# Respacing the side steps of a fused attention and feed-forward kernel

## The chip, the cores and the metric

The kernel runs on one core of one Trainium2 chip. The metric is device time in microseconds (us); lower is better. The time before is the median of three runs, 1308.55 us (1306.65 to 1314.96).

The engines in the text: PE (TensorE, matmuls), DVE (VectorE), ACT (ScalarE), POOL (GpSimd) and SP (SyncE, which here only issues transfers). Each works through its own instructions in the order in which the program lists them, and waits where data or a buffer is missing.

## The reference, cut to what matters

Inputs are x (4 x 1024 x 256, float32), attention weights, and ternary feed-forward weights w1, w2 (1024 x 256), h1, h2 (1024 x 1024) and w3 (256 x 1024) with a scale for each output.

```python
x = x + layernorm(attention(layernorm(x)))      # 16 heads of 16, softmax over 1024 keys
x = x + layernorm(ffn(layernorm(x)))

def attention(x):
    q, k, v = split(x @ Wqkv.T)
    scores = q @ k.T / sqrt(16)
    e = exp(clip(scores - max(scores), -50, 50))
    return ((e / (sum(e) + 1e-6)) @ v) @ Wout.T

def ffn(x):
    h = silu(x @ w1.T * w1s) * (x @ w2.T * w2s)
    h = gelu(h @ h1.T * h1s)
    h = gelu(h @ h2.T * h2s)
    return h @ w3.T * w3s
```

The small term 1e-6 stands beside a sum of exponentials relative to the row's maximum. The kernel takes exponentials without subtracting the maximum, so it needs the largest exponential of each row: these are the "maxima" below.

## The kernel before

**Attention.** The 16 heads form NG = 4 groups of 4 heads, and the 1024 queries form NH = 2 halves of NQ = 512. The list `tiles` runs over batch b, group g, half h, block c of 128 keys (NT = 8), and u, a pair of heads. That makes 512 tiles. For each tile PE makes the scores s of two heads (128 keys by 2 x 512) and ACT takes their exponential into a ring of RING = 8 tiles (`exponentials`). For each two tiles PE multiplies by the values into acc (`weigh`; one such pair is a block of the weighing), and DVE keeps a running maximum in `top` (`rise`). Sixteen tiles make one unit (b, g, h).

At the end of a unit (`unit_end`) DVE copies acc to `o`, and `divide` brings the maxima into the form that the division needs: SP sends `top` to DRAM (`top_d`), SP brings it back folded over more partitions (`back`, tile `folded`), DVE reduces it further (`fold`), and PE and DVE transpose `o` and divide (`run`; PE writes the one bank `misc`, whose next user must wait until DVE has read it).

**Turns.** The main loop goes by turns of TURN = 3 tiles: three score tiles, then one or two blocks of weighing (so that the number alternates), then one call of `side.take`. All other work of attention is cut into `Step`s in chains that `Side` holds. A step has a gap: it is taken at the earliest that many turns after the step ahead of it in its chain. In one `take`, at most one step with matmuls (`tensor`) is taken over all chains, and chains are asked in order, those of the unit ends first. A unit's chain is added before the take of its own turn, so a gap of 1 means that turn. A `heavy` step is one with a projection; a `patient` one isn't taken right after another heavy step. `next_is_heavy` lets the loop hold back a second block of weighing where a heavy step is due and the ring has room.

**The chains.**

- `prologue(b + 1)` works ahead for the next batch: layernorm (`norm`), normalised rows and their transposes into xT (`xt`), projections to q and k of the first 8 heads (`qk[0]`), values (`v`), then q and k of the last 8 heads (`qk[1]`, not patient there). The results go to the tiles `cq`. `flags` steps compute bounds that decide whether a slower general kernel has to run afterwards.
- `stack(b, g)` copies one group's rows of `cq` (high and low halves) into the operands of the score matmuls, `sk` for keys and `sq` for queries: 32 transfers on SP, for the group after the next. The call comes at the end of a group's half 1. `few` packs several transfers into one step with a gap of 1. `outstanding` lists stacks that aren't complete, and `later["qk1"]` is the batch whose last 8 heads are projected.
- `load_rest` loads later batches of x, wo and the scales, on SP, behind the first stack.
- `round_weights` reads the feed-forward weights, rounds them on POOL and stores them; SP loads them back at the end of attention (`load_weights`), w1, w2 and w3 into the `cq` tiles that have become free.
- `ending(b, h)` follows the last unit of a half: transposes, the projection by wo (py, tile y), layernorm and the residual sum. For the last unit it also calls `open_ffn`, which takes the feed-forward buffers and loads h2.

SP's queue is strictly in order. The lines that matter: stack copies are issued at L418, `top_d` at L505, `folded` at L508, later weights at L740. The fold is L512 on DVE, the transposes of `o` L517 and of `folded` L520 on PE. Score matmuls are L470, exponentials L471, weighing L478, maxima L487, the division L492 to L495. Projections (p, pv, py) are matmuls at L264, copies out of PSUM are L267 (ACT) and L270 (DVE), and transposes are L306 (pt) and L555.

**Feed-forward.** Eight halves go through `gated` (w1, w2), `gelu_layer` (h1, then h2) and `finish` (w3). The first calls `side.take` after each of its 8 column blocks, which is where the last units' endings are done.

Of the kernel before, what the change touches and what calls it, by code (L numbers as in the profile page):

```python
# [116 lines left out]
def tile_fast(ctx: ExitStack, tc: tile.TileContext, x, wqk, wv, wo, w1, w1s, w2, w2s, h1, h1s, h2, h2s, w3, w3s, out, bad):  # L117
# [62 lines left out]
    with ExitStack() as actx, ExitStack() as rctx:  # L180
# [91 lines left out]
        def prologue(b, space, copy):  # L272
# [122 lines left out]
                    nc.vector.tensor_scalar(misses[0:1, k + i : k + i + 1], most[:, i : i + 1], limit, 0.0, ALU.is_le, ALU.is_equal)  # L395

            norm = [[Step(gather(h, i), 1, False) for i in range(0, TPQ, 2)] + [Step(root(h), 0, False)] for h in range(NH)]
            xt = [[Step(apply(h, i), 1, False) for i in range(0, TPQ, 2)] + [Step(transposes(h, c), 1) for c in range(DC)] for h in range(NH)]
            qk = [[[Step(project(w, m, h), 1, heavy=True) for w in (1, 0)] for h in range(NH)] for m in range(DC)]
            v = [Step(values(t), 1, heavy=b > 0) for t in range(0, NT, 2)]  # L400
            flags = []
# [19 lines left out]

            return [copy(u, j, n) for u in range(2) for j in range(PARTS) for n in range(2)]

        def few(run_all, n=5):


            def some(part):
                return lambda: [run() for run in part]

            return [Step(some(run_all[i : i + n]), 1, False, quiet=True) for i in range(0, len(run_all), n)]  # L430

        def stack(b, g):

            outstanding.append((b, g))

            def done():
                stacked[g % 2] = b, g
                outstanding.remove((b, g))

            steps = few([lambda copy=copy: copy(nc.sync) for w in (1, 0) for copy in copies(g, w)])  # L440
            steps[0].ready = lambda: g < GPT or later["qk1"] == b
            return steps + [Step(done, 0, False, quiet=True)]

# [56 lines left out]
        def divide(g, h, o, top):  # L500


            there = shuffle.tile([HPG, P, P], F32, tag="top", name="top_d")
            folded = work.tile([P, P // SLOT, P], F32, tag="folded", name="folded", bufs=1)
            nc.sync.dma_start(out=there.rearrange("i k q -> k i q"), in_=top.rearrange("p u n q -> p (u n) q"))  # L505

            def back():
                nc.sync.dma_start(out=folded, in_=there.rearrange("i (k s) q -> (i k) s q", s=P // SLOT))  # L508

            def fold():  # L510
                for n in (2, 1):
                    nc.vector.tensor_max(folded[:, 0:n], folded[:, 0:n], folded[:, n : 2 * n])  # L512

            def run():
                p = misc("po")
                for t in range(TPQ):
                    nc.tensor.transpose(p[:, t * P : (t + 1) * P], o[:, t * P : (t + 1) * P], ident)  # L517

                pm = p.rearrange("p (n s) -> p n s", s=SLOT)[:, :, HOLE : HOLE + P // (TPQ * HPG)]
                nc.tensor.matmul(pm, folded[:, 0], ident.rearrange("p (n k) -> p n k", n=TPQ * HPG), start=True, stop=True, is_transpose=True)  # L520
                em = small.tile([P, HPG], F32, tag="em", name="em")
                nc.vector.tensor_reduce(em, pm.rearrange("p (i n) k -> p i n k", i=HPG), AX.XY, ALU.max)
                po = p.rearrange("p (t i s) -> p t i s", t=TPQ, s=SLOT)
                quotients(g, h, em, po)

            return [Step(back, 1, False, quiet=True), Step(fold, 2, False), Step(run, 1)]

        def divide_last(g, h, o, top):

# [14 lines left out]
        def ending(b, h, copy):  # L544

            st = {}

            def transposes(c):
                def run():
                    if c == 0:  # L550
                        st["oT"] = work.tile([P, DC, NQ], F32, tag="oT", name=f"oT_{b}_{h}", bufs=1)
                        st["y"] = (both if h else work).tile([P, TPQ, D], F32, tag="y", name=f"y_{b}_{h}", bufs=1)
                    pt = misc(f"po_{b}_{h}_{c}")
                    for t in range(TPQ):
                        nc.tensor.transpose(pt[:, t * P : (t + 1) * P], on[h][:, t, c * P : (c + 1) * P], ident)  # L555
                    copy(st["oT"][:, c, :], pt)

                return run

            def project(t0):  # L560
                def run():
                    py = misc(f"py_{b}_{h}_{t0}").rearrange("p (t d) -> p t d", d=D)
                    for i in range(2):
                        for c in range(DC):
                            by_slots(py[:, i, :], st["oT"][:, c, (t0 + i) * P : (t0 + i + 1) * P], wo_sb[:, c, :], start=c == 0, stop=c == DC - 1)
                    (copy if b == B - 1 else to_scalar)(st["y"][:, t0 : t0 + 2, :], py)

                return run

            def gather(i):  # L570
                def run():
                    st["mv"] = norms.gather([st["y"][:, j, :] for j in range(i, i + 2)], i, st.get("mv"))

                return run

            def root():
                st["ln"] = norms.root(st["mv"])

            def apply(i0):
                def run():  # L580
                    for i in range(i0, i0 + 2):
                        norms.apply(st["y"][:, i, :], st["y"][:, i, :], st["ln"], i)

                return run

            def residual(i):
                def run():
                    xr = xs[b][:, h * TPQ + i : h * TPQ + i + 2, :]
                    nc.vector.tensor_add(xr, xr, st["y"][:, i : i + 2, :])

                return run

            return (
                [Step(transposes(c), 1) for c in range(DC)] + [Step(project(t), 2 if t else 1, heavy=True) for t in range(0, TPQ, 2)]
                + ([Step(open_ffn, 0, False)] if (b, h) == (B - 1, NH - 1) else [])
                + [Step(gather(i), 1, False) for i in range(0, TPQ, 2)] + [Step(root, 0, False)]
                + [Step(apply(i), 1, False) for i in range(0, TPQ, 2)] + [Step(residual(i), 1, False) for i in range(0, TPQ, 2)]
            )
# [90 lines left out]
        def unit_end(b, g, h):  # L689

            o = both.tile([P, NQ], F32, tag="o", name="o", bufs=2)
            to_vector(o, accs[b, g, h])

            assert g or not b or not any(step.tensor for step in ends[b - 1, h][0])
            unit = side.add((divide_last if (b, g) == (B - 1, NG - 1) else divide)(g, h, o, tops[b, g, h]), True)
            if g == NG - 1:
                last = ending(b, h, to_scalar if (b, h) == (B - 1, NH - 1) else to_vector)
                for step in last:
                    step.patient = False
                unit[0].extend(last)  # L700
                ends[b, h] = unit
            if h < NH - 1:
                return

            n, at = g + 2, b
            if n >= NG:
                n, at = n - NG, b + 1
            if b == B - 1 and g == NG - 2:
                side.add([Step(lambda c=c: load_weights("h1", [c]), 2 if c else 0, False, quiet=True) for c in range(HC // 2)])
            if at < B:  # L710
                put = Step(slots(at, n), 0, False)
                if at > b:
                    assert later["qk"] == at
                    later["chain"][0].append(put)
                else:
                    put.run()
                side.add(stack(at, n))
            if g == NG - 3 and b + 1 < B:
                later["chain"][0].extend(later["rest"])
            elif g == NG - 3:  # L720
                chunks = [(n, [c]) for n in ("w1", "w2") for c in range(DC)] + [("w3", range(c, c + 4)) for c in range(0, HC, 4)]
                side.add([Step(lambda n=n, c=c: load_weights(n, c), 2, False, quiet=True) for n, c in chunks])
                side.add([Step(lambda: None, 7, False)] + prepare(0, to_vector))
            if g == NG - 1:
                begin(b + 1)
# [16 lines left out]
        def open_ffn():  # L742
# [3 lines left out]
            ffn["b"] = halves(fb, "hb")  # L746
            homes["h2"] = [fb.tile([P, HID], F32R, name=f"h2_{c}") for c in range(HC)]
            load_weights("h2")

        def norm_steps(tiles, st):  # L750

# [227 lines left out]
        early = [v[1], Step(slots(0, 0, 0, NT // 2), 0, False)]  # L979
        side.add(early + v[2:] + [Step(slots(0, 0), 0, False), Step(slots(0, 1), 0, False)] + sum(qk[1], []) + [Step(lambda: later.update(qk1=0, v=0), 0, False), Step(lambda: add_flags(flags[0] + flags[1]), 0, False)])  # L980
        begin(0)
        side.add(stack(0, 1) + few(load_rest(), 4))
        side.add([s for k in blocks for s in round_weights(*k)])
        made = seen = weighed = 0

# [7 lines left out]
        while weighed < len(tiles):  # L993
            n = end = made
            end += TURN
            make(end)
            if made == len(tiles):
                n = made
# [16 lines left out]
            make(end)  # L1015
            if weighed < len(tiles):
                left = 2 * (NT - tiles[weighed][3])
                side.take(left <= min(4, made - weighed))

        load_weights("h1", range(HC // 2, HC))  # L1020
# [239 lines left out]
```

## Time and profile before

| what | us |
|---|---|
| median of three runs | 1308.55 |
| lowest, highest | 1306.65, 1314.96 |
| the profiled execution, own time | 1312.02 |
| its span, first to last instruction | 1310.2 |
| PE busy | 1247.4 |
| ACT busy | 723.2 |
| DVE busy | 701.3 |
| POOL busy | 118.0 |

The granted PE clock is 0.987 on the mean. Attention lasts to about 635 us, and the feed-forward part takes the rest. A row of a timeline gives start, length, engine and source line, the operation, its output and inputs by tile name, the shapes and a count; a bracket at its end holds the engine's idle time just ahead of it and what ended it. "SPq" is SP's queue issuing a transfer. A row of the stretches gives the window, its length, and for each engine its busy time and count, then PE's granted clock, the busy share of the transfer engines, and GB/s. A row of waits gives the waiting engine, tile and line, what it waited for, the total in us, how many times, and the longest.

### The profile page before, as it was taken

To read this page: it belongs to the slowest core of one execution; us is meant where nothing else is said; L and a number is where in the kernel's file an instruction comes from. 1 tells how busy PE (TensorE), PEld (TensorE's weight loads), DVE (VectorE), ACT (ScalarE), POOL (GpSimd) and SP (SyncE) were. 2 spreads that over 40 slices of the span, in tenths; PEclk is the share of its full clock that TensorE was granted. 3 is DMA by queue.
4 is the path that set the end of the run, shared out by engine and by line. 5 is a ranking of instruction groups with operands and counts; after the bars stand their busy time and mean duration, and the time that the engine had idled before them with its cause. 6 is when DMAs were issued, how large, how long until landed. Compare 5 with 4: busy or idle time off the path is not lost.

```text
span 1310.2 us, 21118 instructions
## 1 busy us (share of the span) xinstructions
PE 1247.4 (95%) x8104; PEld 770.6 (59%) x8104; DVE 701.3 (54%) x1578; ACT 723.2 (55%) x902; POOL 118.0 (9%) x166
## 2 busy tenths in 40 slices
PE   7997999999999999988999999999999999999995
PEld 3332333333333333323588888888888888888885
DVE  3364457764487445646663634647446474463533
ACT  3886889889898988988521422314223142231410
POOL 6220113112030000000000000000000000000000
PEclk8998999999999999999999999999999999999998
DMA  4674556566554444455220000201102011020000
GB/s 128 175 225 111 149 137 171 146 143 176 117 146 97 88 98 98 84 121 167 81 113 1 25 1 1 65 25 33 57 1 65 25 33 57 1 65 9 17 1 20
DMA packets 65678, 107.02 MB, mean 82 GB/s; under 512 B 12960, under 2 KB 39200, under 8 KB 65568
## 3 DMA queue, kind: packets, MB, share of 16 engines
q1 hardware_dynamic: 57680, 80.93, 25.2%
q0 software_dynamic: 7360, 24.12, 5.9%
q8 instruction: 66, 1.08, 0.4%
q10 hardware_dynamic: 528, 0.52, 0.1%
q14 instruction: 44, 0.36, 0.1%
HBM read 48.38 MB, written 23.59 MB: 55 GB/s over the span
## 4 chain that ended last, share of the span: by engine, by line
PE 68%; DVE 10%; DMA 7%; ACT 6%; SPq 5%; issue 2%; ACTq 0%; POOL 0%; POOLq 0%; DVEq 0%
PE ph L796 36%; PE acc L478 10%; PE s L470 7%; SPq L418 5%; PE pz L849 4%; ACT e L471 4%; PE pg L796 3%; PE p L264 3%; DMA folded<-top_d 3%; PE py L264 2%; DVE sg L812 2%; DMA top_d<-top 2%; DVE ha_lo L801 1%; PE pv L264 1%; DVE st L95 1%
## 5 line engine op out<-in xcount | busy, mean ns | idle before, releaser
L471 ACT ACTIVATE e<-s 128x1024 f32<-128x1024 f32 x512 | 483.9, 1036 | 45.7 <-PE s L470 26.2
L478 PE MATMUL acc<-e,vaug 128*32 128x512 f32 x2048 | 257.4, 605 | 0.9 <-POOL vaug L448 0.7
L832 ACT ACTIVATE a<-ph,h_scale 128x512 f32<-128x512 f32 x128 | 81.0, 685 | 300.9 <-PE ph L796 300.9
L470 PE MATMUL s<-sq,sk 64*128 64x512 f32 x1024 | 186.0, 446 | 18.7 <-ACT e L471 12.6
L796 PE MATMUL ph<-hb_hi,h 128*128 128x512 f32 x512 | 199.5, 390 | 0.0
L796 PE MATMUL ph<-hb_lo,h 128*128 128x512 f32 x512 | 199.4, 390 | 0.0
L470 PEld LDWEIGHTS s<-sq,sk 64*128 64x128 f32 x1024 | 86.2, 186 | 137.1 <-ACT e L471 108.5
L487 DVE TENSOR_TENSOR top<-top,e 128x512 f32<-128x512 f32 x192 | 135.3, 705 | 18.3 <-ACT e L471 12.2
L478 PEld LDWEIGHTS acc<-e,vaug 128*32 128x32 f32 x2048 | 49.5, 109 | 108.3 <-issue 104.1
L105 POOL TENSOR_TENSOR rstd<-ve,minus_half 128x4 f32<-128x4 f32 (+1 forms) x33 | 36.8, 1114 | 793.3 <-DVE ve L103 793.3
L796 PEld LDWEIGHTS ph<-hb_lo,h 128*128 128x128 f32 x512 | 96.1, 188 | 20.1
L796 PEld LDWEIGHTS ph<-hb_hi,h 128*128 128x128 f32 x512 | 96.1, 188 | 20.2
L833 DVE CAST ha_hi<-a 128x512 fp32r<-128x512 f32 x64 | 27.1, 424 | 141.8 <-ACT a L832 141.8
L796 PE MATMUL ph<-ha_hi,sq 128*128 128x512 f32 x256 | 101.7, 397 | 0.4
L796 PE MATMUL ph<-ha_lo,sq 128*128 128x512 f32 x256 | 99.9, 390 | 0.0
L796 PE MATMUL ph<-ha_lo,sk 128*128 128x512 f32 x256 | 99.8, 390 | 0.0
L796 PE MATMUL ph<-ha_hi,sk 128*128 128x512 f32 x256 | 99.7, 390 | 0.0
L810 ACT ACTIVATE sg<-pg,w_scale 128x512 f32<-128x512 f32 x64 | 43.3, 688 | 55.0 <-DVE ha_lo L801 43.3
L812 DVE SCALAR_TENSOR_TENSOR sg<-pg,w_scale,sg 128x512 f32<-128x512 f32 x64 | 47.1, 745 | 48.3 <-ACT sg L810 48.3
L264 PE MATMUL p<-xT,wqk_sb 128*32 128x512 f32 x512 | 62.4, 609 | 2.5 <-DVE on L495 1.0
L833 DVE CAST hb_hi<-a 128x512 fp32r<-128x512 f32 x64 | 27.0, 422 | 69.0 <-ACT a L832 69.0
L796 PEld LDWEIGHTS ph<-ha_hi,sq 128*128 128x128 f32 x256 | 48.1, 188 | 12.7 <-DVE sg L812 3.3
(164 smaller groups left out, 1637.2 us busy)
## 6 DMA issues: line engine op xcount, KB each, us to landing
w<-in_h_dram POOLq DMA_DIRECT2D x16, 512.0 KB, 6.4
h_r<-wr POOLq DMA_DIRECT2D x16, 512.0 KB, 4.0
x<-in_h_dram SPq DMA_DIRECT2D x32, 256.0 KB, 2.6
top_d<-top SPq DMA_DIRECT2D x30, 256.0 KB, 2.5
folded<-top_d SPq DMA_DIRECT2D x30, 256.0 KB, 3.2
sk<-ck1hi SPq DMA_DIRECT2D x64, 64.0 KB, 2.7
sk<-ck1lo SPq DMA_DIRECT2D x64, 64.0 KB, 2.5
sq<-cq1hi SPq DMA_DIRECT2D x64, 64.0 KB, 2.4
```

Of the source, the lines that this page charges most:

```text
L264: nc.tensor.matmul(o[j : j + SLOT, :], w[:, j : j + SLOT], i, **flags)
L418: queue.dma_start(out=stacks[w, i, u][o : o + DH, c0:c1].bitcast(F32), in_=cq[w, m, k][r : r + DH, c0:c1].bitcast(F32))
L470: nc.tensor.matmul(s[:, a, :], stacks[1, g % 2, u][r, c * P : (c + 1) * P], stacks[0, g % 2, u][r, h * NQ : (h + 1) * NQ], start=True, sto ...
L471: nc.scalar.activation(pair(k)[:, u], s, AF.Exp)
L478: nc.tensor.matmul(acc[SLOT * i : SLOT * (i + 1), :], vaug[g % 2][:, c, i, :], pair(k)[:, i // 2, i % 2, :], start=c == 0, stop=c == NT - 1)
L487: nc.vector.tensor_max(top, top if c > 1 else pair(k - 2)[:, :, :, 0:P], pair(k)[:, :, :, 0:P])
L796: nc.tensor.matmul(p, homes[n][c][:, m * P : (m + 1) * P], half[:, c, :], start=c == 0 and k == 0, stop=c == len(homes[n]) - 1 and k == 1)
L810: nc.scalar.activation(sg, p[:, 0, :], AF.Silu, scale=scales["w1"][:, m : m + 1])
L812: nc.vector.scalar_tensor_tensor(sg, p[:, 1, :], scales["w2"][:, m : m + 1], sg, ALU.mult, ALU.mult)
L832: nc.scalar.activation(a, p[:, j, :], AF.Gelu, scale=scales[n][:, m : m + 1])
L833: nc.vector.tensor_copy(o[0][:, m, :], a)
L849: nc.tensor.matmul(p[t], half[:, c, t * P : (t + 1) * P], homes["w3"][c], start=c == 0 and k == 0, stop=c == HC - 1 and k == 1)
```

## The change

- The transposes into xT come two turns after the normalisation (first of each half), not one; the first projection by wo comes two turns after the transposes, not one.
- A stack's 32 copies go by 4 in a step, not 5, or by 6 where the last 8 heads of the batch are needed and not yet projected when the stack is called for. `load_rest` goes by 1 in a step, not 4.
- `back` comes a turn later.
- What was an assertion on the first unit of the next batch becomes a condition on its `run`: it waits for the matmul steps of the ending of the batch before.
- w1's loads wait until the flag steps are done, w2's until no stack is outstanding, and w3's move into `open_ffn`, behind those of h2.
- After a turn that weighed two blocks or more, patient heavy steps aren't taken.

```diff
-  xt = ... [Step(transposes(h, c), 1) for c in range(DC)]
+  xt = ... [Step(transposes(h, c), 1 if c else 2) for c in range(DC)]

   # stack(b, g)
-  steps = few([... for w in (1, 0) for copy in copies(g, w)])              # n=5
+  steps = few([... for w in (1, 0) for copy in copies(g, w)], 4 if g < GPT or later["qk1"] == b else 6)

   # divide
-  return [Step(back, 1, False, quiet=True), Step(fold, 2, False), Step(run, 1)]
+  return [Step(back, 2, False, quiet=True), Step(fold, 2, False), Step(run, 1)]

   # ending
-  [Step(project(t), 2 if t else 1, heavy=True) for t in range(0, TPQ, 2)]
+  [Step(project(t), 2, heavy=True) for t in range(0, TPQ, 2)]

   # unit_end
-  assert g or not b or not any(step.tensor for step in ends[b - 1, h][0])
   unit = side.add(..., True)
+  if b and not g:
+      unit[0][-1].ready = lambda: not any(step.tensor for step in ends[b - 1, h][0])
   ...
-  chunks = [(n, [c]) for n in ("w1", "w2") for c in range(DC)] + [("w3", range(c, c + 4)) for c in range(0, HC, 4)]
-  side.add([Step(lambda n=n, c=c: load_weights(n, c), 2, False, quiet=True) for n, c in chunks])
+  chunks = [(n, [c]) for n in ("w1", "w2") for c in range(DC)]
+  loads = [Step(lambda n=n, c=c: load_weights(n, c), 2 if n == "w1" else 1, False, quiet=True) for n, c in chunks]
+  loads[0].ready = lambda: not later["flags"][0]
+  loads[DC].ready = lambda: not outstanding
+  side.add(loads)

   # open_ffn
   load_weights("h2")
+  load_weights("w3")

-  side.add(stack(0, 1) + few(load_rest(), 4))
+  side.add(stack(0, 1) + few(load_rest(), 1))

   # the loop over turns
+  before = weighed
   ...
+  side.tired = side.tired or weighed - before >= 4
   side.take(left <= min(4, made - weighed))
```

More of the change, by code (lines that the diff above doesn't have):

```diff
@@ L397, in prologue @@
             norm = [[Step(gather(h, i), 1, False) for i in range(0, TPQ, 2)] + [Step(root(h), 0, False)] for h in range(NH)]
-            xt = [[Step(apply(h, i), 1, False) for i in range(0, TPQ, 2)] + [Step(transposes(h, c), 1) for c in range(DC)] for h in range(NH)]
+            xt = [[Step(apply(h, i), 1, False) for i in range(0, TPQ, 2)] + [Step(transposes(h, c), 1 if c else 2) for c in range(DC)] for h in range(NH)]
             qk = [[[Step(project(w, m, h), 1, heavy=True) for w in (1, 0)] for h in range(NH)] for m in range(DC)]
@@ L422, in copies, with few @@
             return [copy(u, j, n) for u in range(2) for j in range(PARTS) for n in range(2)]
-        def few(run_all, n=5):
+        def few(run_all, n):
             def some(part):
@@ L438, in done @@
                 outstanding.remove((b, g))
-            steps = few([lambda copy=copy: copy(nc.sync) for w in (1, 0) for copy in copies(g, w)])
+            steps = few([lambda copy=copy: copy(nc.sync) for w in (1, 0) for copy in copies(g, w)], 4 if g < GPT or later["qk1"] == b else 6)
             steps[0].ready = lambda: g < GPT or later["qk1"] == b
@@ L593, in ending @@
             return (
-                [Step(transposes(c), 1) for c in range(DC)] + [Step(project(t), 2 if t else 1, heavy=True) for t in range(0, TPQ, 2)]
+                [Step(transposes(c), 1) for c in range(DC)] + [Step(project(t), 2, heavy=True) for t in range(0, TPQ, 2)]
                 + ([Step(open_ffn, 0, False)] if (b, h) == (B - 1, NH - 1) else [])
```

## The prediction

> **What bounds the kernel now.** I read the busy rows first, then the busy time by stretches, the chain of waits, the list of waits, and the timeline round the longest stops. A *unit* below is one (batch, group, half); it is over when its 16th tile is weighed. "h0" and "h1" are its two halves.
>
> ```profile
> PE 1247.4 (95%) x8104; PEld 770.6 (59%) x8104; DVE 701.3 (54%) x1578; ACT 723.2 (55%) x902; POOL 118.0 (9%) x166
> PE   7997999999999999988999999999999999999995
> ACT  3886889889898988988521422314223142231410
> ```
> ```profile
> 80.00:120.00 40.00, 31.17 (x218) 10.90 (x214) 19.19 (x40) 28.53 (x34) 4.78 (x6) 0.87 0.64 164
> 280.00:320.00 40.00, 38.07 (x374) 15.27 (x372) 20.40 (x48) 36.54 (x44) 7.41 (x11) 1.00 0.66 163
> 680.00:720.00 40.00, 40.00 (x190) 33.52 (x189) 13.05 (x26) 8.09 (x13) 0.00 (x0) 1.00 0.00 0
> ```
> There are two regimes. From 635 us on (feed-forward) PE has no gap (40.00 of 40), and the change hardly touches that part. From 27 to 632 us (attention) PE and ACT are both near full (38.1 and 36.5 of 40 at 280), so a stop of either is lost to the end. The stretch at 80 is the poorest: both engines lose 7 to 8 us against 280, and PE's granted clock is 0.87 there.
>
> ```profile
> PE ph L796 36%; PE acc L478 10%; PE s L470 7%; SPq L418 5%; PE pz L849 4%; ACT e L471 4%; PE pg L796 3%; PE p L264 3%; DMA folded<-top_d 3%; PE py L264 2%; DVE sg L812 2%; DMA top_d<-top 2%; DVE ha_lo L801 1%; PE pv L264 1%; DVE st L95 1%
> ```
> ```profile
> DVE folded L512 <- DMA folded<-top_d: 41.3, 15, 7.7
> PE po L520 <- DVE folded L512: 12.0, 4, 7.8
> PE s L470 <- DMA sq<-cq1lo: 2.8, 1, 2.8
> ```
> The chain passes through SP's issue of stack copies (L418, 5%), then through the maxima's way out (top_d, 2%) and back (folded, 3%). DVE stands 41.3 us for the maxima, and PE 12.0 us behind DVE. The timeline shows how:
>
> ```profile
> 100.94 2.49 SPq L418 DMA_DIRECT2D sq<-cq1lo  x4
> 103.48 0.58 SPq L418 DMA_DIRECT2D sq<-cq1hi  x1
> 104.16 0.53 SPq L505 DMA_DIRECT2D top_d<-top  x1
> 106.73 0.33 SPq L508 DMA_DIRECT2D folded<-top_d  x1
> 109.60 0.75 DVE L512 TENSOR_TENSOR folded<-folded 128x256 f32<-128x256 f32 x2 [7.67 <-DMA folded<-top_d]
> 110.40 0.47 PE L520 MATMUL po<-ident,folded 128*128 128x128 f32 x1 [7.79 <-DVE folded L512]
> 111.69 2.85 ACT L471 ACTIVATE e<-s 128x1024 f32<-128x1024 f32 x3 [7.55 <-issue]
> 112.38 3.56 PE L478 MATMUL acc<-e,vaug 128*32 128x512 f32 x16
> ```
> The unit (b0, g1, h0) was done at 92.64 (copy of acc to o), yet SP sent top_d only at 104.16, behind a row of copies at 0.62 us each (2.49 / 4). In all 15 h0 units that were profiled with top_d, SP sent it 0.1 to 11.5 us after o (median 3.0); in the 15 h1 units 2.7 us before to 0.6 after. SP's queue is late in h0 units only, because the 32 copies of the next stack start at the h1 end before them.
>
> **What the stops cost.** I sorted the 170 turns by what PE does in them and took the median of each kind; a turn's excess is its length less that median. Excesses at the stops of the maxima: (b0,g0,h0) 0.93 + 1.05 = 1.98; (b0,g1,h0) 11.58 against 3.75, then 5.66 against 3.57, = 9.92; (b0,g2,h0) 5.27 against 3.45 = 1.82 (PE waits for DVE's read of the misc bank, DVE for folded, 5.33). For (b3,g1,h0) the neighbours without projections give 5.79 per two turns: 9.28 - 5.79 = 3.49. The sum is 17.2. The last stack's late landing (below) took 7.88 for two such turns: 2.09. Together **19.3 us**. ACT's idle at the same places is 1.81 + 1.44, 7.55 + 2.55, 1.90, 1.94 + 1.02 and 1.57, 19.8 us, so no other engine gained meanwhile and I count it in full.
>
> After the 7.79 us gap the next 16 acc matmuls took 3.50 us to the next instruction, against 1.85 elsewhere; after the 2.20 us gap at 557 they took 2.56. Both are inside the excesses. The Trainium skill ("TensorE: Matmul & The Clock Gate", What's actually happening) has PE's clock halved after about 3.4 us idle. By that rule the second would not be slow; the trace has it slow, and by the rule the sum would be 0.7 less.
>
> **The change, part by part.**
>
> *Stacks by 4 a turn (6 only where a batch's second half of q and k is not ready at the call).* The same 32 copies, 0.63 us each. Five turns (mean (631.94 - 27.27) / 170 = 3.56 us) lie between the h1 end and the next h0 end. Before, 25 copies stood ahead of top_d there; now 20 do: 5 x 0.63 = 3.15 us earlier, which is the median lateness. Four a turn need 2.5 us of a turn's 2.75 to 3.6; five needed 3.15. The case of six: only b1's fourth projection (PE at 235.7) falls in the turn of the unit end, so one stack (b1,g2); its unit (b1,g1,h0) stays as late as now, its excess of 0.82 is not in my sum.
>
> *The rest of the loads by 1 a turn, not 4.* Between 79.45 and 104.16 the queue also held 11 of these transfers (2 of wo, 4 of x, 5 of scales) beside the copies. Now each turn holds one step (0.57 us for a wo piece): 20 x 0.63 + 5 x 0.57 = 15.5 from 77.1 gives 92.6, when the maxima are ready. 25 steps from turn 9 on end near 30 + 34 x 3.56 = 150 us; wo is first used at 199.6, x of batch 2 after 200. Nothing is late.
>
> *back a turn later.* back, fold and run go from turns 0, 2, 3 after the end to 1, 3, 4. On SP, 4 copies (2.5 us) now stand between top_d and back, which hides top_d's landing (2.5 us) instead of blocking the queue. On DVE, fold comes 3.56 us later. Ready: o + 0.8 + 0.5 + 2.5 + 0.4 + 3.2 (at most 5.4) = 7.4 to 9.6 us after the end; wanted: three turns, 8.7 to 10.7. So DVE's 41.3 us goes to at most 1 us in a few units, and PE, a turn behind fold, feels none. run then ends 4 turns after the end, before the next unit's 5.33; the o, top and folded buffers are not needed sooner.
>
> *xt transposes, and the first y projection, gap 2; the ready condition on the next batch's first run.* The same instructions a turn later. Removed: PE's waits there, 0.10 + 0.47 + 0.17. The prologue has slack: b3's q and k were projected by 425, wanted at 460. The next batch's first run comes 15 turns after the ending starts, so its condition is already true. At the end, the last y projections move up to two steps into the first gate stage, and with them the eight h2 loads (landed 667.7, wanted at 688): two steps of 2.3 to 3.9 us are covered. Price 0.
>
> *No patient heavy step in a turn of two blocks.* Of ten heavy steps behind two blocks in the trace, one (59.2) is patient; the others are second-half q/k, y and batch 0's v. PE's work is the same; -0.5 to +0.5, taken as 0.
>
> *w1, w2, w3.* Before, w2's load stood in the middle of the last stack:
>
> ```profile
> 593.34 0.33 SPq L740 DMA_DIRECT2D cq1hi<-w_r  x1
> 593.71 1.14 SPq L418 DMA_DIRECT2D sq<-cq1lo  x2
> 598.50 0.93 PE L470 MATMUL s<-sq,sk 64*128 64x512 f32 x4 [2.77 <-DMA sq<-cq1lo]
> ```
> It overwrites cq, so it waited for copies to land, and two copies waited behind it. Now w2 waits until no stack is outstanding: copies go out by 583.5 + 0.5 + 2.5 + 0.4 + 2.5 = 589.4 and land near 592, before 595. That is the 2.09. w2 is wanted at 635 and comes near 600. w3's eight loads follow h2's: 8 x 0.48 after 660, wanted at 717. Hidden by the h1 layer.
>
> *What it may cost anew.* Every moved step meets other neighbours on DVE and in the one misc bank. PE's gaps behind late DVE work (norm, xT, on, oT, ck0lo), beside those counted, are ten, 8.2 us in all. The change could clear them all (+8.2) or add as many (-8.2). No row says which; I take two new ones of 1 us: -2.0.
>
> **Sum:** 19.3 - 2.0 = 17.3 us. The profiled execution took 1312.02 (span 1310.2, 1.8 around it), so 1294.7; the median of the runs shown is 3.5 lower, 1308.55, and gives **1291.2**. (1%, 13.1 us, is about what a measurement of this kernel can tell from no change.)
>
> **Rivals.**
> - *A wait takes the place:* fold and run fall on busier DVE turns and the 8.2 us of late DVE gaps double. 19.3 - 8.2 = 11.1: 1297.5. For it: four such gaps at po L517 already lie beside maxima that came in time. Against: fold itself no longer blocks DVE.
> - *The maxima still land late:* half the stops stay: 19.3 / 2 - 2.0 = 7.7: 1300.9. For it: folded took 5.1 to 5.4 us in four units while 512 KB loads ran. Against: that fits in three turns. The Trainium skill ("DMA: Bandwidth & Descriptors", Issuing engines are not separate DMA queues) speaks for it: transfers of all issuers share the same 16 engines, so four copies sent behind top_d slow it. The trace agrees in that top_d, 2.5 us in the middle, took 4.6 at 600 with large loads in flight.
> - *Slower: stacks land late.* The last four copies come in the eighth turn, not the seventh. The first s of a group found its stack landed only 0.70 to 3.87 us before (14 groups, 33.7 in all). If landing slips by one turn and half of back's stop (5.0 us), PE stands 14 x 5.0 - 33.7 = 36.3 us: 1291.2 + 36.3 = 1327.5. It decides from a slip of 3.6 us (17.1 us of stops). Against: SP isn't paced by turns; copies run at 0.63 us each, and by the count above they end sooner.
> - *More than counted:* the 8.2 us goes as well: 25.5: 1283.0. For it: (b1,g0,h0) had 1.72 of excess behind fold's 0.96.
>
> **How the numbers follow.** Forecast 0.48 (own range 1285 to 1298), a wait in its place 0.20, late maxima 0.12, late stacks 0.10, more 0.10. Faster by over 1% (under 1295.5): 0.85 x 0.48 + 0.10 + a quarter of 0.20 = 0.56. Slower by over 1%: late stacks and a little, 0.11. Within: 0.33. The range reaches below the best case (1283) and to the late maxima with the 8.2 us added (1300.9 + 8.2): 1281 to 1309.
>
> **What would show it.** Right: DVE's wait for folded under 8 us in all, no PE wait at L520, top_d of h0 units sent within 1 us of o, the window 80 to 120 at clock 1.00 and 37 us of PE, no wait of s for sq<-cq1lo, the feed-forward part as long as before (675 us). Wrong: first s of groups waiting for sk or sq; po L517 or py waiting for DVE by more than 15 us; the attention part ending after 625 us.

## The result, and the profile after

The changed kernel takes 1303.33 us (median, 1300.64 to 1306.56), the kernel before 1308.22 us on the same chip. The ratio is 0.9956, 95% interval 0.9942 to 0.9970: a gain of 4 to 8 us, real but within 1%. The prediction was 1291.2, a gain of 17.3. The profiled execution took 1304.9 us with a span of 1303.1, so between the two profiles the span lost 7.1.

First the busy rows, the stretches and the chain of the kernel after. In the feed-forward part its source lines lie 6 further down.

```profile
PE 1246.2 (96%) x8104; PEld 771.5 (59%) x8104; DVE 700.2 (54%) x1578; ACT 721.6 (55%) x902; POOL 119.4 (9%) x166
```
```profile
80.00:120.00 40.00, 35.41 (x258) 12.63 (x248) 20.47 (x42) 32.96 (x38) 7.11 (x9) 0.91 0.61 142
280.00:320.00 40.00, 39.17 (x362) 15.15 (x360) 20.64 (x47) 37.70 (x45) 7.58 (x10) 1.00 0.65 162
```
```profile
PE ph L802 36%; PE acc L478 12%; ACT e L471 8%; PE s L470 8%; PE pz L855 4%; PE pg L802 4%; PE p L264 4%; PE py L264 2%; PE pv L264 2%; DVE sg L818 2%; PE po L517 1%; DVE ha_lo L807 1%; DVE top L487 1%; DVE st L95 1%; ACT sg L816 1%
```
SP's copies (5% of the chain before), top_d (2%) and folded (3%) no longer stand among the chain's largest lines: of the stop that the change attacks, little is left in what sets the end. The stretch at 80 is better (PE 31.2 to 35.4 of 40) but not well: its granted clock is still 0.91.

The list of waits (engine, tile and line, what it waited for: total us, times, longest us) shows what is left and what is new:

```profile
DVE folded L512 <- DMA folded<-top_d: 12.5, 5, 5.4
PE po L517 <- DVE cq0lo L330: 3.6, 1, 3.6
PE po L555 <- DVE oT L270: 2.0, 1, 2.0
PE s L470 <- DMA sq<-cq1lo: 1.9, 1, 1.9
PE py L264 <- DVE norm L362: 1.7, 1, 1.7
```
DVE's wait for the maxima fell from 41.3 to 12.5 us, and PE's 12.0 us at L520 is gone. In its place PE waits for DVE at transposes and projections: 3.6, 2.0 and 1.7 us here, and 1.6, 1.4 and 1.2 in rows further down. The row of s is the stack of (b0, g3), which landed late.

**Where the time went, group by group.** I cut attention at the first score matmul of each of the 16 groups. From batch 1 on such a length hardly varies where the order of the work is the same: the kernel after and experiment e3 below, which differ in batch 0 alone, agree within 0.04 us in all twelve, e15 and e17 in ten. A few times it jumped all the same (against e8, b3 g1 by 1.7 in e13 and e14, and b1 g3 by 1.3 in e14), so a difference of one group below 2 us is used only where several kernels show it. The first gate matmul of the feed-forward part comes at 635.46 us before and 628.68 after; from there to the end it is 674.8 and 674.4.

| us after less before | g0 | g1 | g2 | g3 |
|---|---|---|---|---|
| batch 0 | -2.72 | -6.63 | -1.43 | **+4.27** |
| batch 1 | +0.12 | +0.85 | -1.94 | -1.11 |
| batch 2 | **+2.81** | **+2.91** | -1.59 | +1.14 |
| batch 3 | -0.01 | -1.04 | +0.71 | -2.35 |

The five groups in which the prediction placed its 19.3 us (b0 g0 to g2, b3 g1, b3 g3) gained 14.2. The other eleven lost 8.2, where it had 2.0. Batch 0 gained 6.5 in all, and batches 1 to 3 nothing (+0.5).

Two stops of the kernel after show why. The first is the old one, still there in the worst unit (timeline; "SPq" rows are issues):

```profile
87.51 0.69 DVE L270 TENSOR_SCALAR o<-acc 128x512 f32<-128x512 f32 x1 [0.29 <-PE acc L478]
97.83 0.53 SPq L505 DMA_DIRECT2D top_d<-top  x1
100.46 0.36 SPq L508 DMA_DIRECT2D folded<-top_d  x1
103.24 0.75 DVE L512 TENSOR_TENSOR folded<-folded 128x256 f32<-128x256 f32 x2 [5.37 <-DMA folded<-top_d]
104.07 0.69 DVE L330 SCALAR_TENSOR_TENSOR cq0lo<-p,cq0hi 128x512 fp32r<-128x512 f32 x1
104.82 1.12 PE L517 MATMUL po<-ident,o 128*128 128x128 f32 x4 [3.57 <-DVE cq0lo L330]
```
The copy to o was at 87.51 (first row), so top_d of (b0, g1, h0) went 10.3 us late, with 30 stack copies ahead of it. DVE stood 5.37 us in fold; cq0lo, which frees the misc bank, was queued behind; PE stood 3.57 us for the bank.

The second is new, at the start of batch 2, where no transfer is late:

```profile
363.26 1.21 DVE L349 TENSOR_REDUCE sum<-ck1hi 128x1 f32<-128x1024 f32 x1
364.99 0.42 DVE L95 BATCH_NORM_STATS2 st<-y 128x6 f32<-128x256 f32 x1
366.26 0.69 DVE L270 TENSOR_SCALAR oT<-po 128x512 f32<-128x512 f32 x1
367.00 0.66 PE L555 MATMUL po<-ident,on 128*128 128x128 f32 x4 [2.04 <-DVE oT L270]
372.76 0.75 DVE L512 TENSOR_TENSOR folded<-folded 128x256 f32<-128x256 f32 x2
373.54 0.69 DVE L362 TENSOR_REDUCE norm<-pn 64x4 f32<-64x512 f32 x1
374.29 1.94 PE L264 MATMUL py<-wo_sb,oT 128*32 128x256 f32 x32 [1.68 <-DVE norm L362]
```
The layernorm of y (st<-y) of the ending, the next batch's sums and norm, and a fold fall together on DVE. oT stands behind sum and st, norm right behind a fold (before, this fold ended 0.7 us ahead of norm). Each PE step there needs the misc bank that DVE has yet to read (oT, norm), and waits.

### The profile page after: what moved, and what is told of

Read it like the earlier page. It is cut to its first block, busy times and chain, and to the rows that moved or that the text cites. A ratio compares the mean times of both kernels' runs of the same rounds, so it can differ in the third digit from the quotient of the medians.

```text
span 1303.1 us, 21108 instructions
## 1 busy us (share of the span) xinstructions
PE 1246.2 (96%) x8104; PEld 771.5 (59%) x8104; DVE 700.2 (54%) x1578; ACT 721.6 (55%) x902; POOL 119.4 (9%) x166
## 3 DMA queue, kind: packets, MB, share of 16 engines
q8 instruction: 66, 1.08, 0.3%
## 4 chain that ended last, share of the span: by engine, by line
PE 74%; ACT 10%; DVE 8%; issue 3%; DMA 2%; POOL 1%; SPq 1%; ACTq 0%; POOLq 0%; DVEq 0%
PE ph L802 36%; PE acc L478 12%; ACT e L471 8%; PE s L470 8%; PE pz L855 4%; PE pg L802 4%; PE p L264 4%; PE py L264 2%; PE pv L264 2%; DVE sg L818 2%; PE po L517 1%; DVE ha_lo L807 1%; DVE top L487 1%; DVE st L95 1%; ACT sg L816 1%
## 5 line engine op out<-in xcount | busy, mean ns | idle before, releaser
L470 PE MATMUL s<-sq,sk 64*128 64x512 f32 x1024 | 189.5, 447 | 22.2 <-ACT e L471 17.2
L818 DVE SCALAR_TENSOR_TENSOR sg<-pg,w_scale,sg 128x512 f32<-128x512 f32 x64 | 47.1, 745 | 46.3 <-ACT sg L816 46.1
```

The lines of the kernel that those rows point to most:

```text
L470: nc.tensor.matmul(s[:, a, :], stacks[1, g % 2, u][r, c * P : (c + 1) * P], stacks[0, g % 2, u][r, h * NQ : (h + 1) * NQ], start=True, sto ...
L818: nc.vector.scalar_tensor_tensor(sg, p[:, 1, :], scales["w2"][:, m : m + 1], sg, ALU.mult, ALU.mult)
```

## The experiments

The theory after the result: the maxima's later return is the gain; the y projection's gap takes it back in batches 1 to 3; the rule on two blocks delays a stack in batch 0. Rivals: the gain is the spreading of transfers; the loss is late stacks, or shared transfer engines. All ratios are to the kernel before on the same chip, with their 95% intervals. "Lengths" are those of groups, from the profiled execution.

**1. What brings the gain?** The extra turn alone taken out of the changed kernel (e7), and alone put into the kernel before (e8):

```diff
-            return [Step(back, 2, False, quiet=True), Step(fold, 2, False), Step(run, 1)]
+            return [Step(back, 1, False, quiet=True), Step(fold, 2, False), Step(run, 1)]    # e7; e8 is the reverse, in the kernel before
```


> The changed kernel with the bringing back of the maxima in the unit's own turn again. Theory (the extra turn is what takes the wait off DVE): folded lands 7.4 us after the unit's end at best and fold asks for it after two turns, 5.8 to 7.1, so DVE waits in most h0 units again (10 to 20 us in all), the copies stand behind the landing of the maxima, and the time rises by 3 to 8 us. Rival (with 4 copies a turn SP is in time anyway, the turn was not needed): within 2 us of the changed kernel, or faster, since the division comes a turn sooner.

> The kernel before with nothing but the maxima brought back a turn later. Theory: fold asks 3.6 us later, more than the median lateness of 3.0, so DVE's 41 us of waiting falls to about 10, PE's stop at (b0, g1, h0) from 7.8 to 4, the other stops of PE vanish, and the time falls by 6 to 10 us. Rival (five copies now stand between sending and bringing back, so the maxima come back as late against fold as before): DVE still waits 25 us or more, and the time stays within 3 us.

Measured: e7 1314.92, ratio 1.0022 (1.0000 to 1.0043); e8 1299.22, ratio 0.9907 (0.9873 to 0.9941). The waits of e7, then those of e8:

```profile
DVE folded L512 <- DMA folded<-top_d: 28.9, 10, 8.5
PE po L520 <- DVE folded L512: 8.6, 1, 8.6
```
```profile
DVE folded L512 <- DMA folded<-top_d: 22.1, 7, 6.4
PE po L517 <- DVE xT L270: 4.5, 1, 4.5
```
The one number in `divide` is worth about 12 us alone (e8), twice the whole change, and about 9 us within it (1.0022 less 0.9956); all the rest together, without it, is worth nothing or a little less. DVE still stands 22.1 us in e8, yet PE no longer stands at L520: with one more turn the wait of DVE is absorbed before PE needs it. (For e8, a wait of about 10 us and a gain of 6 to 10 were foretold: the wait fell less and the gain was larger.) That settles against the spreading of transfers as the source.

**2. The gaps.** Both gaps back to 1 in the changed kernel (e4), the xt gap alone back (e5); on top of e8, the xt gap alone (e9), or the projection's gap alone with the ready condition that it needs (e10).

```diff
-... [Step(transposes(h, c), 1 if c else 2) for c in range(DC)]          # e4, e5
+... [Step(transposes(h, c), 1) for c in range(DC)]                      # e9: the reverse, in e8
-... [Step(project(t), 2, heavy=True) for t in range(0, TPQ, 2)]         # e4
+... [Step(project(t), 2 if t else 1, heavy=True) ...]                   # e10: the reverse, in e8
```


> The changed kernel with the gaps of the xT transposes and of the first y projection back at 1. Bunching theory: the moved ending now puts the layernorm of y on DVE in the same turns as the next batch's own layernorm, PE waits behind DVE for the one misc bank (2.0, 1.7, 1.6 and 1.4 us between 365 and 397), and the groups from b2g0 and b2g1 lose 2.8 and 2.9 us. With the gaps back both return to 38.8 and 34.3 us and the time falls by 3 to 6 us. Rival (the later maxima move the ending, not these gaps): both groups stay at 41.6 and 37.3, and the time stays within 2 us.

> The changed kernel with the gap of the xT transposes alone back at 1 (the first y projection stays at 2). With both back the time fell from 0.9956 to 0.9890 of the kernel before, by 8.6 us. Theory of the ending: it is the y projection, a turn later in all eight endings, that puts the layernorm of y beside the next batch's work, and the xT gap acts once a half: at most 2 us here, ratio 0.994 to 0.996. Rival theory of the prologue: the xT gap delays the projections of q and k, and the whole 8.6 us comes back, ratio 0.989.

> The kernel before with the maxima brought back a turn later (that alone gave 0.9907, a span of 1298.2 us) and the xT transposes at gap 2. If this gap is what the whole change lost: the time rises by 3 to 8 us, ratio 0.993 to 0.997. If it is harmless, as the forecast had it (the prologue has slack): within 2 us of 0.9907.

> The kernel before with the maxima a turn later, and the first y projection at gap 2 (with the ready condition that it needs). If the later ending is what meets the next batch's work on DVE: the groups from b2g0 and b2g1 grow by 2 to 3 us each against 38.5 and 35.9, and the time rises by 3 to 8 us. If harmless: within 2 us of 0.9907.

| | ratio (95%) | batch 0, us | batches 1 to 3, us |
|---|---|---|---|
| before | 1 | 164.5 | 443.7 |
| the change | 0.9956 (0.9942 to 0.9970) | 158.0 | 444.2 |
| e4, both gaps undone | 0.9890 (0.9869 to 0.9911) | 150.7 | 438.7 |
| e8, back only | 0.9907 (0.9873 to 0.9941) | 159.9 | 436.6 |
| e9 = e8 + xt gap | 0.9897 (0.9868 to 0.9926) | 157.4 | 436.3 |
| e10 = e8 + projection gap | 0.9938 (0.9916 to 0.9959) | 158.7 | 442.4 |

e10 loses 5.8 us in batches 1 to 3 against e8, at the start of the batches (b1 g0 +1.18, b2 g1 +1.24, b3 g0 +1.08, b3 g1 +0.84), where an ending lies beside the next batch's prologue. Each of these is small, and less than the 2 to 3 us foretold for b2 g0 and b2 g1 (+0.5 and +1.2), but the total stands over all runs: the six kernels with `back` at 2 and the projection's gap at 2 (the change, e1, e2, e3, e5, e10) take 442.4 to 444.4 us in batches 1 to 3, the twelve with it at 1 take 436.3 to 440.7. Undoing both gaps in the changed kernel (e4) gives 5.5 back there, 2.0 and 2.3 of it in b2 g0 and b3 g0.

Group b2 g1 did not follow e4's expectation: it stays at 37.0 (37.25 in the change, 34.3 before). Part of its loss comes with the turn itself (35.9 in e8) and part with the rule on two blocks, which the prediction took as 0: with the projection's gap at 1, b2 g0 and b2 g1 take 39.6 to 39.7 and 37.0 in the four kernels with the rule (e4, e6, e12, e18), and 38.2 to 38.5 and 35.3 to 36.1 in the eight without it. Other groups shorten with the rule (b2 g2 by about 1 us), so its price over these batches is not settled.

The xt gap costs nothing on top of e8 (e9). In the changed kernel the evidence is split. By its times e5, with the xt gap alone undone, is as fast as e4: 1299.24, ratio 0.9898 (0.9865 to 0.9932), which is what the rival foretold. Its profiled execution, however, was the slowest of its eight (1306.06), and in it batches 1 to 3 take 444.4, as in the changed kernel, so no trace shows where the others were faster. The loss in batches 1 to 3 goes with the projection's gap (e9, e15, e16 and e17 have the xt gap at 2 and take 436.3 to 436.9); whether the xt gap costs something more in the changed kernel stays open.

In e10's list of waits stand many short ones of PE for DVE's readings of the misc bank (p for norm 1.6, xT 1.3 and oT 1.2, py for xT 1.1). Over batches 1 to 3 PE stands 3.0 us longer in e10 than in e8 (21.5 and 18.5), 2.7 of it behind DVE, and ACT 5.0 longer (48.2 and 43.2). So half of the 5.8 is read directly as PE waiting for DVE; the other half lies in turns that are longer without a gap that the trace gives to anyone, and no run splits it further.

**3. Batch 0: who sends the maxima late?** In the changed kernel, stacks always by 4 (e1), no rule on two blocks (e2), the rest by 4 again (e3); on top of e8, the rule alone (e12) and the rest by 1 alone (e13).

```diff
-            steps = few([...], 4 if g < GPT or later["qk1"] == b else 6)
+            steps = few([...], 4)                                        # e1
-                side.tired = side.tired or weighed - before >= 4         # e2 (e12: added to e8)
-        side.add(stack(0, 1) + few(load_rest(), 1))
+        side.add(stack(0, 1) + few(load_rest(), 4))                      # e3 (e13: the reverse, in e8)
```


> The changed kernel, with every stack's copies by 4 a turn (never 6). Queue theory: in the changed kernel the stack for (b0, g2) went by 6, because the two-block rule moved the last q/k projection of batch 0 past the unit end; so 30 copies stood ahead of the maxima of (b0, g1, h0), sent 10.3 us late, and DVE stood 5.4 us, PE 3.6, ACT 4.9. With 4 a turn they leave 6 us earlier, DVE's wait there is under 1 us, the group from b0g1's first scores to b0g2's is 3 to 5 us shorter, and the time falls by 3 to 5 us (about 1299). Rival (the stop only moves): the stack of (b0, g2) lands after its first score matmul, and the time stays at 1303.

> The changed kernel without the rule that keeps patient heavy steps out of turns with two blocks. The projection of batch 0 is then done before the unit end again, so that stack goes by 4 of itself. Queue theory: the same gain as with 4 always, 3 to 5 us. Rival (the rule earns its keep elsewhere): the time stays or rises, since turns with two blocks and a projection (4.5 us against 2.75 and 3.6 apart) come back.

> The changed kernel with the remaining loads by 4 a turn again, not 1. Queue theory: spread by 1 they run beside the stacks of (b0, g2) and (b0, g3), and made the latter land 2.9 us after its first score matmul; by 4 they are over by then, the group that begins at b0g3 loses its extra 4.3 us, but the maxima of the first batch's units are sent later again by 4 loads a turn: net -3 to +2 us. Rival (the loads do no harm): the group from b0g3 stays at 40 us.

> The kernel before with the maxima a turn later, and the rule of no patient heavy step in a turn of two blocks. There is no six-a-turn rule here for it to set off. If its harm in the whole change came only from that: within 2 us of 0.9907. If keeping large steps out of full turns is worth something: 2 to 4 us faster; if it delays the projections: slower by as much.

> The kernel before with the maxima a turn later, and the remaining loads by 1 a turn. If spreading them is what helps the first batch: DVE's wait for folded falls below 15 us (22.1 without it), the group from b0g1 falls under 42, and the time is 1 to 4 us below 0.9907. If the loads only move beside later stacks: one of the groups from b0g2 and b0g3 grows by as much, within 2 us of 0.9907.

| | ratio (95%) | (b0, g1), us | (b0, g3), us |
|---|---|---|---|
| the change | 0.9956 (0.9942 to 0.9970) | 41.1 | 40.0 |
| e1, always by 4 | 0.9915 (0.9899 to 0.9932) | 37.1 | 39.1 |
| e2, no rule | 0.9919 (0.9901 to 0.9938) | 36.9 | 37.8 |
| e3, rest by 4 | 0.9964 (0.9952 to 0.9975) | 46.1 | 35.8 |
| e8, back only | 0.9907 (0.9873 to 0.9941) | 43.5 | 36.9 |
| e12 = e8 + rule | 0.9907 (0.9876 to 0.9938) | 48.0 | 35.7 |
| e13 = e8 + rest by 1 | 0.9888 (0.9851 to 0.9924) | 39.5 | 36.8 |

The rule kept batch 0's last q and k projection past the end of the unit (b0, g0, h1), so `stack(0, 2)` was called with the last 8 heads not projected and went by 6. That put 30 copies ahead of top_d, not 20. Without the rule the stack goes by 4 of itself, and SP sends top_d 5.5 us earlier (timeline of e2):

```profile
92.29 0.39 SPq L505 DMA_DIRECT2D top_d<-top  x1
```
e1 reaches the same by the other way. Either gives about 5 us (0.9956 less 0.9915 or 0.9919, of 1308). With stacks by 4 the rule itself costs nothing in (b0, g1) (e1 keeps it, e2 does not), so there its price comes with the stack. On top of e8 the rule nets nothing in time (e12): (b0, g1) is 4.5 longer, but by another stop, that of (b0, g0, h1), whose folded took 8.0 us to land while PE stood 7.9 us; other groups are shorter. The rest by 1 does what was foretold in (b0, g1): 5.0 us in the changed kernel (e3), 4.0 on top of e8 (e13). But against e3 the changed kernel gives 4.2 us back in (b0, g3): by 1, the loads stretch over the next stack too. That does not happen always: with the loads by 1 too, (b0, g3) takes 35.7 in e4 and 36.8 in e13. DVE's wait for the maxima in e13, foretold below 15 us, stayed at 21.6.

**4. Stacks by 4, and the weights' loads.** On top of e8, stacks by 4 (e11, `n=4`), the new conditions of the loads (e14), both with the xt gap (e16); and in the changed kernel, always by 4 with both gaps undone (e6), and the projection's gap and the rule undone (e15).

```diff
-        def few(run_all, n=5):
+        def few(run_all, n=4):                                           # e11, e16, in e8
+                loads[0].ready = lambda: not later["flags"][0]           # e14, e16, with w3 in open_ffn
+                loads[DC].ready = lambda: not outstanding
-                side.tired = side.tired or weighed - before >= 4         # e15, with project(t), 2 if t else 1
```


> The kernel before with the maxima a turn later, and stacks by 4 copies a turn, not 5. Queue theory: DVE's wait for folded falls from 22.1 us to under 8, PE's stop of 4.5 us behind it at 106 goes, the group from b0g1 falls from 43.5 to about 39, and the time falls by 3 to 5 us, ratio about 0.987. Rival (the later stack takes it back): first score matmuls of a group wait for sk or sq, and the time stays within 2 us of 0.9907.

> The kernel before with the maxima a turn later, and w1, w2 and w3 loaded as in the changed kernel. The wait of 2.8 us for the last stack that the forecast gave to these loads is already gone with the maxima alone (the group from b3g3 is 37.5 us in both), so nothing is left to gain: within 2 us of 0.9907. If the loads do matter by themselves: 2 us faster or more, in the groups from b3g2 and b3g3.

> The kernel before with the maxima a turn later, stacks by 4, the xT gap at 2 and the new loads of w1, w2, w3; the remaining loads stay at 4 a turn. If the spread by 1 earns nothing and the parts add: 0.987 to 0.989, as the kernel without the y projection's gap and the two-block rule, and the candidate for the fastest. If the 4 a turn stand ahead of the maxima of (b0, g1, h0) as before: the group from b0g1 stays above 42 and the time at 0.991.

> The changed kernel with both gaps back at 1 and stacks always by 4. If the two losses have separate causes they add: 8.6 us and 5.3 us (0.9956 to 0.9915), ratio 0.985, about 1289, which is the 17 to 19 us that the forecast had for the stops alone. Rival (both cure the same late stack of the first batch): the sum is short by the 4.3 us that either run gets back in the group from b0g3, ratio 0.988.

> The changed kernel without two of its parts: the y projection's gap back at 1, and no two-block rule. If these two are what the change lost (4 us by the one alone, 4 to 5 by the other through the stack by 6): ratio 0.987 to 0.989, near the 17 us of the forecast. If more is lost elsewhere: 0.991 or above.

| | median, us | ratio (95%) | batch 0, us | batches 1 to 3, us |
|---|---|---|---|---|
| e11 | 1296.40 | 0.9892 (0.9862 to 0.9921) | 156.9 | 439.0 |
| e14 | 1300.00 | 0.9918 (0.9888 to 0.9949) | 159.0 | 439.5 |
| e16 | 1296.26 | 0.9892 (0.9858 to 0.9927) | 157.5 | 436.9 |
| e6 | 1298.01 | 0.9898 (0.9862 to 0.9933) | 156.7 | 440.7 |
| e15 | 1296.65 | 0.9891 (0.9853 to 0.9928) | 157.1 | 436.4 |

In e11 w2 is loaded over cq before the last copies of the last stack are out, so its last group computes with other numbers; the work is the same. It shows what the new conditions are for: they go with stacks by 4. By themselves they gain nothing (e14: b3 g3 37.58 us, e8 37.53). Gains don't add: e6 joins e1 and e4, was foretold at 0.985, and ends no faster than e4 alone; in e6 (b0, g3) takes 40.0 us again (35.7 in e4), and batches 1 to 3 take 2.0 more.

e15 is the change without its two costly parts. With e4, e9, e11, e13 and e16 it lies at 0.989, 1295 to 1297 us; the intervals don't part these six, but all end below the 0.9942 at which the change's begins. Leaving out e11, whose numbers are others, the five beat both kernels.

**5. SP's queue or the shared engines?** In e15 (e17) and e6 (e18) the loads of `load_rest` go through POOL's queue.

```diff
-                return lambda: nc.sync.dma_start(out=out, in_=in_)
+                return lambda: nc.gpsimd.dma_start(out=out, in_=in_)
-                return lambda: load_x(b, [h])
+                return lambda: load_x(b, [h], nc.gpsimd)
```


> The kernel of e15 (the change without the y projection's gap and the two-block rule), with the remaining loads issued by POOL, not SP. If SP's queue in batch 0 is what still holds the maxima and the stacks of b0g2 and b0g3 (the landing of 1.3 and 1.5 us after the first scores, 4.2 us of DVE wait in e15): the groups from b0g2 and b0g3 fall from 39.2 and 40.1 to 36 to 37, and the time to 0.984 to 0.987. If it is the shared transfer engines, not the queue: both groups stay, and the time at 0.989.

> The kernel of e6 (the change with both gaps at 1 and stacks always by 4, two-block rule kept), with the remaining loads issued by POOL. If SP's queue is the cause of e6's late stack (b0g3 at 40.0 us): that group falls to 36, and the time from 0.9898 to 0.984 to 0.987. If the transfer engines are: no change.

Measured: e17 1300.35, ratio 0.9926 (0.9908 to 0.9945), no better than e15 (its span is 1.5 longer, though attention is 1.2 shorter; the last section has the rest); e18 1299.85, 0.9920 (0.9902 to 0.9937), no better than e6. The timeline of e17:

```profile
88.01 0.53 SPq L505 DMA_DIRECT2D top_d<-top  x1
93.03 0.34 SPq L508 DMA_DIRECT2D folded<-top_d  x1
125.93 0.36 SPq L505 DMA_DIRECT2D top_d<-top  x1
134.09 0.34 SPq L508 DMA_DIRECT2D folded<-top_d  x1
```
With SP's queue free of loads, top_d of (b0, g1, h0) went at 88.01 beside o at 87.90: on time, and the length of (b0, g2) fell from 39.2 to 36.7. But top_d of (b0, g2, h0) took 8.1 us to land (4.3 in e15, 2.3 in the middle), so `back` waited at the head of SP's queue until 134.09; the copies behind it were late, the next stack landed 4.15 us after its first score matmul, and (b0, g3) lost 2.5. Neither expectation came in full: what the free queue gave in (b0, g2), one late landing took back in (b0, g3), and in e18 (b0, g3) stays at 40.0. POOL issued five loads of x and weights between 123.35 and 126.55, and a landing slowed by them agrees with the Trainium skill ("DMA: Bandwidth & Descriptors", Issuing engines are not separate DMA queues): transfers of all issuers meet at the same engines. That the loads are the cause is argued, not shown: the engines were 73% busy in these 8.1 us, and 100% in e15's 4.3.

## Why the prediction was right and wrong, point by point

- **The mechanism: right.** The maxima's return a turn later is the gain (e7, e8). As foretold, no PE wait is left at L520, and top_d of the h0 units goes at o: the median lateness is 0.02 us (3.0 before), under 1 us in 12 of 15, and (b1, g1, h0), named as staying late, has 3.0. The forecast of at most 1 us of DVE's wait was wrong: 12.5, of which 5.4 is the one unit above.
- **The 19.3 us of stops: a size.** In the groups named, 14.2 came. Foretold and found: (b0, g0) 1.98 and 2.72, (b0, g1) 9.92 and 6.63, (b0, g2) 1.82 and 1.43, (b3, g1) 3.49 and 1.04, (b3, g3) 2.09 and 2.35. The largest shortfall is (b0, g1), for which failed step 2 has the reason; of the one of (b3, g1), 2.45, up to 1.7 may be the jump seen there.
- **Failed step 1: "xt transposes, and the first y projection, gap 2 ... Price 0".** True of xt on top of e8 (e9; open in the changed kernel, e5), false of y: 5.5 (e4) to 5.8 (e10) in batches 1 to 3. I counted the PE waits that it removes (0.74 us) and who needs the y rows, not what follows them: the layernorm of y goes a turn later too, onto other DVE turns of the next batch's prologue, and PE's next users of the misc bank queue behind it. The term for new waits, -2.0 between +8.2 and -8.2, should have held this. The eleven groups not named lost 8.2 net, so the rival "a wait takes the place" was right in kind; its price, 8.2, was for other places.
- **Failed step 2: "no patient heavy step in a turn of two blocks ... taken as 0" with "one stack (b1, g2)" by 6.** The rule costs about 5 us because it moves a projection past the call of a stack, which then takes the other branch of the change (e1, e2). I costed the two edits apart; they meet. I had seen the one patient step that the rule would move (59.2), but not that the step behind it in its chain then slips past the unit's end. The working by which SP is free for top_d at 92.6, when the maxima are ready, fell with it (97.83, for an o at 87.51).
- **Late stacks happened once.** The stack of (b0, g3) landed at 147.38, after its first score matmul at 144.45, and that group lost 4.3. The signs for the other 14 that it would have needed are absent. So that rival was a mishap of one group and not its 36 us.
- **Transfers.** The rest by 1 gave 4.0 to 5.0 in (b0, g1), as foretold, but I did not follow the loads into the next stack, where the changed kernel loses 4.2 against e3. The last stack's 2.09 fits the group (2.35) by luck: on top of e8 the new conditions give nothing (e14), and e8, without them, has the same length there, so the gain comes with `back`.
- **The other signs.** Window 80 to 120: clock 0.91 for 1.00, PE 35.4 for 37. Feed-forward: 674.4 for 675. End of attention: 628.7, past the 625 named as wrong. PE's waits at po L517 and py: 6.4 us in all, under the 15 named; the loss sits in many places, under the size I looked for. The 1% named there as what a measurement can tell from no change was too coarse: the change's 0.4% lies clear of it (0.9942 to 0.9970).

Of the 12.1 us between forecast and measurement, e15 gives back 0.0065 of 1308, 8.5 us, by undoing the two failed steps; the two intervals leave 2 to 15. The rest fits the late stack and the interplay in batch 0, which no run here parts further.

## What to carry to other kernels

Where a fast engine stands behind a slow round trip, moving the return by one slot was worth more than speeding the road to it; try that one number alone before spreading the rest. A step that is moved takes with it all that follows in its chain: list which engine the followers fall on and what else is there in that turn, and price a bank that two engines hand to and fro by every reader that comes later. And where an edit sets a branch (a stack by 4 or by 6) and another moves the event that decides it, work out the two together.

## What the runs showed of the hardware that was not expected

- **A gap and the clock.** Four transposes of one shape took 0.66 us after a gap of 2.04 us at 367.00 and 1.12 us after one of 3.57 us at 104.82. For these two the trace agrees with the Trainium skill ("TensorE: Matmul & The Clock Gate", What's actually happening), which has the clock halved after about 3.4 us idle. Other gaps don't follow it: the granted clock was 0.50 from 559.5 to 562.8 in the kernel before, behind a gap of 2.20 us, and 0.50 from 147.9 to 151.1 in the kernel after, behind one of 1.93, but 1.00 from 598.5 to 602.0 in the kernel before, behind one of 2.77. So the length of the gap alone doesn't decide; what does stays open.
- **Landing times.** The same transfer, top_d, landed after 2.5 us in the middle before the change and 2.3 after it; the longest were 4.6 before, 5.6 after and 8.1 in e17, with the transfer engines 68%, 98% and 73% busy during them.
- **The end of e17.** With the loads on POOL's queue, the program closed 10.7 us after DVE's last operation, in e17 and e18 alike; it was 8.0 to 8.2 in the kernels before and after, e6 and e15. So about 2.6 us of e17's and e18's times lie there and not in attention. No run tells why.
